# Joint block transposes, GpSimd reciprocals and a head-by-head latent layer in a four-layer transformer kernel

## The chip, the cores and the metric

The kernel runs on one core of a Trainium2 chip. The metric is the device time of one execution in microseconds (us); the time of a kernel is the median of its runs. The engines are named as the profile names them: PE (TensorE, matmuls), PEld (its weight loads), DVE (VectorE), ACT (ScalarE), POOL (GpSimd) and SP (SyncE, which here only issues DMAs).

## The reference, cut to what matters

Two sequences of 1024 tokens with 128 features pass through four layers, each an attention and a feed-forward part with residuals, all in float32:

```python
x = x + attn_a(layernorm(x));  x = x + mx_ffn(layernorm(x))     # one shared key/value head, no mask
x = x + attn_b(layernorm(x));  x = x + mx_ffn(layernorm(x))     # 16 heads, causal
x = x + attn_c(layernorm(x));  x = x + moe(layernorm(x))        # latent keys/values of 32, causal
x = x + attn_d(layernorm(x));  x = x + moe(layernorm(x))        # 16 heads with biases, causal
# every attention: 16 heads of 64
attn = softmax(q @ k.T / 8, axis=-1);  out = (attn @ v) @ w_o
```

The softmax over the keys of each query is where the change lies: maximum, exponential with its sum, reciprocal of the sum, product with it, transpose, product with the values.

## The kernel before

**Units and steps.** The four layers are called a, b, c and d. A unit is one pair of heads of one batch, so each layer has 16 units. A unit is worked through in steps. In layer a a step is one tile of 128 queries against all 1024 keys (8 steps a unit, 128 in all). In the causal layers a step holds one or two query tiles whose keys together fill 1024 columns or fewer, in the order `[7], [6, 0], [5, 1], [4, 2], [3]` (5 steps a unit, 80 a layer).

**One step.** `scores` (line 638) makes the scores of both heads in PSUM, with two buffers, one for each head; DVE reduces each to its negative maximum (`nmax`, L682); ACT takes the exponential with that bias into the tile `pr` and leaves the sums in `tot` (L693); DVE makes the reciprocals `rec` (L701); POOL multiplies the probabilities by them (L705); DVE transposes them in blocks of 32x32 into `slots` (L775); 16 DMAs (13 in layer a, where ACT and POOL copy three quarters) move the blocks between quarters of the partitions into `prT` (L750); PE multiplies with the values into `av` (L849, in layer c L844). Key tiles that are not block-transposed go through PE (`pp`, L792) and a copy on ACT (L793).

**Order.** Every engine's order is written by hand: the program is recorded in the order of a loop over steps, and each engine runs its instructions in that order. In the iteration of step j the loop does, in this order: the transposes of step j-2, with the normalisation (reciprocal and POOL products) of step j-1 put in after the first transpose; additions of finished outputs to x; scores, maxima and exponentials of step j; some of the next unit's projections; some of the "side" work (norms, feed-forward groups, the next layer's start); and four key tiles of the product with the values. On DVE this makes, for each step: transpose of head 0, reciprocals, transpose of head 1, two or four maxima. A query block's (256 queries) product with the values is released two iterations after its second transpose.

**PE's rows.** In layers a, b and d a product over 64 rows takes half of PE's rows, and each head's scores run as two streams side by side, head 0 first, then head 1. The latent layer's products are over 32 rows. There, four streams run side by side, two for each head, taken in turn, and the masks of both heads follow them:

```python
if latent:
    in_turn([half(h) for h in range(2) for half in (lower, upper)])
    for h in range(2):
        mask(h)
```

Of the kernel before, what the change touches and what calls it, by code (L numbers as in the profile page):

```python
# [9 lines left out]
F32 = mybir.dt.float32  # L10
# [26 lines left out]
def kernel(ctx: ExitStack, tc: tile.TileContext, a: dict, out: bass.AP):  # L37
# [68 lines left out]
    prT_four = probTp.tile([P, 2 * 4 * AB], F32, tag="prT_four", name="prT_four")  # L106
    latT_first = probTp.tile([P, S], F32, tag="latT", name="latT")


    stats = {}  # L110

# [149 lines left out]
    def moe_group(nm, b, g, last, xT, eng=nc.gpsimd, other=None):  # L261
# [3 lines left out]
        if other:  # L265
            xn = qkp.tile([P, TPB, D], F32, tag="qx", name=f"xn_{k}")
            hids = [
                probp.tile([P, 2, S], F32, tag="pr", name=f"hid_{k}_{n}").rearrange(
                    "p h (c q) -> p (h c) q", q=QB
                ) for n in range(2)  # L270
            ]
        else:
            xn = None
# [335 lines left out]
    def keys(u, qt):  # L609
        return qt + 1 if layers[u[0]]["causal"] else NT  # L610

    def step_of(u, qts):
        k = f"{tag_of(u)}_{qts[0]}"
        at = {}
        if len(qts) == 2:
            at = {qts[1]: 0, qts[0]: keys(u, qts[1]) * P}
        else:
            at = {qts[0]: QB - min(QB, keys(u, qts[0]) * P // 2)}
        pr = probp.tile([P, 2, S], F32, tag="pr", name=f"pr_{k}")
        tot = small.tile([P, 2, len(qts)], F32, tag="tot", name=f"tot_{k}")  # L620
        return dict(u=u, qts=qts, at=at, k=k, pr=pr, tot=tot)

    def scores(st):


        u, qts, at, k = st["u"], st["qts"], st["at"], st["k"]
        causal, latent = layers[u[0]]["causal"], layers[u[0]]["kind"] == "latent"
        sc = [ps_s.tile([P, 2 * QB], F32, tag="sc", name=f"sc_{k}_{h}") for h in range(2)]

        def operands(h, half):  # L630
            if latent:
                return QUARTERS[2 * h + half], qT[u][0], kT[u]
            x = 1 if h != half else 0
            return ROWS[half], qT[u][x], kT[u][x]

        def product(h, half, qt, k0, k1, diagonal):
            r, q, kk = operands(h, half)
            yield nc.tensor.matmul(  # L638
                sc[h][:, at[qt] + k0 : at[qt] + k1], lhsT=q[r, qt * P : (qt + 1) * P],
                rhs=kk[r, k0:k1], start=True, stop=not diagonal,  # L640
            )
            d = at[qt] + qt * P
            for f in range(P // DH if diagonal and not latent else 0):
                yield nc.tensor.matmul(  # L644
                    sc[h][:, d + f * DH : d + P], lhsT=unit[r, f, :], rhs=over[r, f, f * DH :],
                    start=False, stop=(f == P // DH - 1),
                )

        def mask(h):

            for qt in reversed(qts):
                d = at[qt] + qt * P
                nc.tensor.matmul(  # L653
                    sc[h][:, d : d + P], lhsT=ident_b, rhs=over_all, start=False, stop=True
                )

        def lower(h):

            yield from product(h, 0, qts[0], 0, QB - at[qts[0]], False)
            if len(qts) == 2:  # L660
                yield from product(h, 0, qts[1], 0, keys(u, qts[1]) * P, True)

        def upper(h):
            mid = QB - at[qts[0]]
            yield from product(h, 1, qts[0], mid, keys(u, qts[0]) * P, causal)

        def in_turn(gens):
            while gens:
                gens = [g for g in gens if next(g, None) is not None]

        if latent:
            in_turn([half(h) for h in range(2) for half in (lower, upper)])
            for h in range(2):
                mask(h)
        nmaxs = []
        for h in range(2):
            if not latent:
                in_turn([lower(h), upper(h)])
            nmax = small.tile([P, len(qts)], F32, tag="nmax", name=f"nmax_{k}_{h}")
            for n, qt in enumerate(qts):  # L680
                c = slice(at[qt], at[qt] + keys(u, qt) * P)
                nc.vector.tensor_reduce(  # L682
                    out=nmax[:, n : n + 1], in_=sc[h][:, c], axis=AX.X, op=ALU.max, negate=True
                )
            nmaxs.append(nmax)
        return sc, nmaxs

    def exponentials(st, h, sc, nmax):

        u, tot = st["u"], st["tot"]  # L690
        for n, qt in enumerate(st["qts"]):
            c = slice(st["at"][qt], st["at"][qt] + keys(u, qt) * P)
            nc.scalar.activation(  # L693
                st["pr"][:, h, c], sc[:, c], AF.Exp, bias=nmax[:, n : n + 1],
                accum_out=tot[:, h, n : n + 1],
            )

    def normalize(st):
        u, pr = st["u"], st["pr"]
        rec = small.tile([P, 2, len(st["qts"])], F32, tag="rec", name=f"rec_{st['k']}")  # L700
        nc.vector.reciprocal(out=rec, in_=st["tot"])  # L701
        for h in range(2):
            for n, qt in enumerate(st["qts"]):
                c = slice(st["at"][qt], st["at"][qt] + keys(u, qt) * P)
                nc.gpsimd.tensor_scalar(  # L705
                    out=pr[:, h, c], in0=pr[:, h, c], scalar1=rec[:, h, n : n + 1], scalar2=1.0,
                    op0=ALU.mult, op1=ALU.mult,
                )

# [26 lines left out]
    def blocks_moved(u, qb):  # L736


        t, src = prT_of(u, qb)[:, : 2 * blocked(u, qb) * AB], blocks_of(u, qb)
        n = src.shape[1] // 4  # L740
        def ends(i, r):
            return t[QUARTERS[r], i * n : (i + 1) * n], src[QUARTERS[i], r * n : (r + 1) * n]

        copied = (1, 2, 3) if layers[u[0]]["kind"] == "shared" else ()
        for i, r in MOVES:
            if i != r or i not in copied:
                o, x = ends(i, r)
                nc.sync.dma_start(out=o, in_=x)  # L750
        for i in copied:
            o, x = ends(i, i)
            if i < 3:
                nc.gpsimd.tensor_scalar(
                    out=o, in0=x, scalar1=1.0, scalar2=1.0, op0=ALU.mult, op1=ALU.mult
                )
            else:
                copies.append((o, x))
        probT[u, qb] = t.rearrange("p (i t h c) -> p t h i c", t=TPA, h=2, i=4)

    def transposes(st):

        u, pr = st["u"], st["pr"]
        for qt in st["qts"]:
            qb, cols = qt // TPA, slice(qt % TPA * P, (qt % TPA + 1) * P)
            nk, nb = keys(u, qt), blocked(u, qb)
            for h in range(2 if nb else 0):
                n = min(nk, nb)  # L770
                dst = blocks_of(u, qb).rearrange(
                    "p (r t h k q) -> p t h k r q", r=4, t=TPA, h=2, q=32
                )[:, qt % TPA, h, :n]
                src = pr[:, h, st["at"][qt] : st["at"][qt] + n * P]
                nc.vector.transpose(  # L775
                    dst,
                    src.rearrange("p (k r q) -> p k r q", r=4, q=32),
                )
                yield
            if nb < nk and nb:  # L780
                o = rest_of(u, qb)[:, qt % TPA].unsqueeze(2)
            elif nb < nk:
                if (u, qb) not in probT:
                    probT[u, qb] = prT_of(u, qb).rearrange("p (h k q) -> p h k q", h=2, q=AB)
                o = probT[u, qb][:, :, :, cols]
            for k0 in range(nb, nk, 2):
                k1 = min(k0 + 2, nk)
                pt = ps_m.tile([P, 2, 2, P], F32, tag="pm", name=f"pp_{tag_of(u)}_{qt}_{k0}")
                for h in range(2):
                    for kt in range(k0, k1):  # L790
                        c0 = st["at"][qt] + kt * P
                        nc.tensor.transpose(pt[:, h, kt - k0, :], pr[:, h, c0 : c0 + P], ident)  # L792
# [11 lines left out]
    def weigh(u, qb, bank, kt, ends):  # L804
# [12 lines left out]
        def moving(h, kt, t0, t1=TPA):  # L817
# [5 lines left out]
            cols = slice(kt * 32, (kt + 1) * 32)  # L823
            return x[:, :, cols] if t1 - t0 == 1 else x[:, :, :, cols]

        def shaped(o, t0, t1=TPA):
            if not blocked(u, qb):
# [405 lines left out]
```

## Time and profile before

| | |
|---|---|
| median of 3 runs | 2314.12 us (2311.34 to 2315.66) |
| span of the profiled execution, first to last instruction | 2309.5 us; its own total is not given apart, the runs stand 1.8 to 6.2 us above it |
| PE busy | 2112.7 us (91%) |
| DVE busy | 1716.0 us (74%) |
| ACT busy | 1491.3 us (65%) |
| POOL busy | 1285.7 us (56%) |
| DMAs `prT<-slots` | 768 of 128 KB, 832 of 112 KB, 768 of 96 KB |

By the first and the last product of scores the layers lie at 20 to 681 us (a), 685 to 1181 us (b), 1183 to 1669 us (c) and 1673 to 2226 us (d). Busy time counts an instruction from its start to its end; matmuls are pipelined, so a busy PE need not be full. DMA issues on SP count as no busy time.

### The profile page before, as it was taken

What the parts mean: (1) busy time and instruction counts of PE and PEld (TensorE: products, weight loads), DVE (VectorE), ACT (ScalarE), POOL (GpSimd) and SP (SyncE); (2) the same over time, 40 slices, a digit from 0 to 9 for tenths busy, and PEclk for the clock granted to TensorE, in tenths of its full rate; (3) what the DMA queues carried; (4) which work ended last, traced back from release to release, by engine and by line L of the source; (5) the groups of instructions that cost most, each with busy time, mean ns of one, the idle gap of its engine ahead of it and who ended that gap; (6) DMA issues with size and microseconds to landing.
All of it is one profiled execution on the core that took longest, in us unless ns stands there. A gap on an engine that the chain in (4) does not pass through costs nothing.

```text
span 2309.5 us, 43436 instructions
## 1 busy us (share of the span) xinstructions
PE 2112.7 (91%) x14833; PEld 1232.0 (53%) x14833; DVE 1716.0 (74%) x2695; ACT 1491.3 (65%) x3340; POOL 1285.7 (56%) x1723
## 2 busy tenths in 40 slices
PE   6999999999998999999987897888889999999986
PEld 2454444444445666666654454444455666656653
DVE  7978999999986876678668877776666566766544
ACT  5777777767765666666665566656666557666552
POOL 4756767767765454455545645555644446544441
PEclk9999999999999999999998889899899999999997
DMA  5666666556676666666655556544665546646450
GB/s 139 145 150 151 154 150 149 135 131 153 149 189 153 151 154 161 164 153 156 150 130 121 121 128 146 130 104 111 162 156 131 125 114 156 162 118 145 110 135 10
DMA packets 144635, 320.45 MB, mean 139 GB/s; under 512 B 48288, under 2 KB 58784, under 8 KB 144416
## 3 DMA queue, kind: packets, MB, share of 16 engines
q1 hardware_dynamic: 144416, 317.67, 58.2%
q8 instruction: 120, 1.97, 0.4%
q14 instruction: 99, 0.81, 0.1%
HBM read 10.27 MB, written 2.10 MB: 5 GB/s over the span
## 4 chain that ended last, share of the span: by engine, by line
PE 49%; DVE 15%; SPq 12%; ACT 10%; DMA 5%; issue 5%; POOL 3%; DVEq 0%; ACTq 0%; POOLq 0%
SPq L750 12%; PE sc_a L638 5%; PE av_a L849 4%; PE av_d L849 4%; DVE slots L775 4%; DMA prT<-slots 4%; PE sc_b L638 4%; PE av_b L849 4%; PE sc_d L638 4%; DVE nmax_a L682 3%; ACT pr_a L693 3%; ACT pr_c L693 3%; PE sc_c L638 3%; DVE nmax_d L682 2%; DVE nmax_c L682 2%
## 5 line engine op out<-in xcount | busy, mean ns | idle before, releaser
L693 ACT ACTIVATE pr_a<-sc_a,nmax_a 128x1024 f32<-128x1024 f32 x256 | 283.2, 1111 | 169.9 <-DVE nmax_a L682 168.0
L705 POOL TENSOR_SCALAR pr_a<-pr_a,rec_a 128x1024 f32<-128x1024 f32 x256 | 284.1, 1123 | 192.9 <-DVE rec_a L701 192.6
L705 POOL TENSOR_SCALAR pr_d<-pr_d,rec_d 128x1024 f32<-128x1024 f32 (+7 forms) x256 | 186.9, 750 | 269.0 <-DVE rec_d L701 268.8
L682 DVE TENSOR_REDUCE nmax_a<-sc_a 128x1 f32<-128x1024 f32 x256 | 298.3, 1204 | 28.0 <-PE sc_a L638 27.6
L705 POOL TENSOR_SCALAR pr_b<-pr_b,rec_b 128x1024 f32<-128x1024 f32 (+7 forms) x256 | 187.3, 752 | 219.9 <-DVE rec_b L701 219.5
L705 POOL TENSOR_SCALAR pr_c<-pr_c,rec_c 128x1024 f32<-128x1024 f32 (+7 forms) x256 | 187.5, 753 | 206.4 <-DVE rec_c L701 206.4
L682 DVE TENSOR_REDUCE nmax_d<-sc_d 128x1 f32<-128x1024 f32 (+7 forms) x256 | 177.1, 747 | 150.2 <-PE sc_d L644 150.2
L693 ACT ACTIVATE pr_c<-sc_c,nmax_c 128x1024 f32<-128x1024 f32 (+7 forms) x256 | 186.5, 739 | 153.5 <-DVE nmax_c L682 123.9
L693 ACT ACTIVATE pr_b<-sc_b,nmax_b 128x1024 f32<-128x1024 f32 (+7 forms) x256 | 186.5, 739 | 146.8 <-DVE nmax_b L682 130.3
L638 PE MATMUL sc_a<-k_a,q_a 64*128 64x512 f32 x512 | 266.8, 631 | 15.0 <-ACT pr_a L693 14.2
L775 DVE STREAM_TRANSPOSE slots<-pr_a 128x896 f32<-128x896 f32 x256 | 278.8, 1093 | 1.7 <-DMA prT<-slots 1.3
L693 ACT ACTIVATE pr_d<-sc_d,nmax_d 128x1024 f32<-128x1024 f32 (+7 forms) x256 | 186.6, 739 | 135.0 <-DVE nmax_d L682 129.5
L638 PE MATMUL sc_a<-k_a,qx_a 64*128 64x512 f32 x512 | 264.1, 631 | 0.0
L682 DVE TENSOR_REDUCE nmax_b<-sc_b 128x1 f32<-128x1024 f32 (+7 forms) x256 | 176.6, 745 | 89.0 <-PE sc_b L644 88.9
L682 DVE TENSOR_REDUCE nmax_c<-sc_c 128x1 f32<-128x1024 f32 (+7 forms) x256 | 176.8, 747 | 84.8 <-PE sc_c L653 84.0
L849 PE MATMUL av_a<-prT,v_a 128*64 128x256 f32 x1792 | 221.4, 386 | 7.5 <-DMA prT<-slots 5.2
L849 PEld LDWEIGHTS av_a<-prT,v_a 128*64 128x64 f32 x1792 | 121.1, 136 | 122.3 <-issue 69.0
L638 PE MATMUL sc_d<-k_d,q_d 64*128 64x512 f32 (+3 forms) x416 | 159.9, 497 | 0.3 <-ACT pr_d L693 0.3
L638 PE MATMUL sc_b<-k_b,q_b 64*128 64x512 f32 (+3 forms) x416 | 159.1, 495 | 1.1 <-ACT pr_b L693 1.1
L638 PE MATMUL sc_d<-kx_d,qx_d 64*128 64x512 f32 (+3 forms) x416 | 154.3, 490 | 0.2
L638 PE MATMUL sc_b<-kx_b,qx_b 64*128 64x512 f32 (+3 forms) x416 | 153.5, 488 | 0.7 <-ACT pr_b L693 0.6
L775 DVE STREAM_TRANSPOSE slots<-pr_b 128x1024 f32<-128x1024 f32 (+3 forms) x128 | 130.5, 1024 | 9.6 <-DMA prT<-slots 9.0
(408 smaller groups left out, 4782.3 us busy)
## 6 DMA issues: line engine op xcount, KB each, us to landing
prT<-slots SPq DMA_DIRECT2D x768, 128.0 KB, 2.3
prT<-slots SPq DMA_DIRECT2D x832, 112.0 KB, 2.2
prT<-slots SPq DMA_DIRECT2D x768, 96.0 KB, 2.1
qx_b<-q_b SPq DMA_DIRECT2D x32, 256.0 KB, 3.5
kx_b<-k_b SPq DMA_DIRECT2D x32, 256.0 KB, 3.4
qx_d<-q_d SPq DMA_DIRECT2D x32, 256.0 KB, 3.6
kx_d<-k_d SPq DMA_DIRECT2D x32, 256.0 KB, 3.5
x<-in_x SPq DMA_DIRECT2D x4, 256.0 KB, 3.7
```

What stands on the lines that cost most here:

```text
L638: yield nc.tensor.matmul(sc[h][:, at[qt] + k0 : at[qt] + k1], lhsT=q[r, qt * P : (qt + 1) * P], rhs=kk[r, k0:k1], start=True, stop=not dia ...
L682: nc.vector.tensor_reduce(out=nmax[:, n : n + 1], in_=sc[h][:, c], axis=AX.X, op=ALU.max, negate=True)
L693: nc.scalar.activation(st["pr"][:, h, c], sc[:, c], AF.Exp, bias=nmax[:, n : n + 1], accum_out=tot[:, h, n : n + 1],)
L705: nc.gpsimd.tensor_scalar(out=pr[:, h, c], in0=pr[:, h, c], scalar1=rec[:, h, n : n + 1], scalar2=1.0, op0=ALU.mult, op1=ALU.mult,)
L750: nc.sync.dma_start(out=o, in_=x)
L775: nc.vector.transpose(dst, src.rearrange("p (k r q) -> p k r q", r=4, q=32),)
L849: nc.tensor.matmul(shaped(av[ROWS[h], n], t0), lhsT=vs[u][:, kt, h, :], rhs=moving(h, kt, t0), start=(kt == 0), stop=(kt == nkt - 1),)
```

## The change

The probabilities of both heads lie interleaved by key tile in `pr` (`[P, key tile, head, 128]` in place of `[P, head, 1024]`). One DVE instruction transposes both heads of a query tile; it replaces two. The reciprocals are made on POOL, as the sums to the power of -1, against a constant tile of -1; the DVE instruction goes away. In the latent layer each head's scores run as two streams on two quarters of PE's rows, followed by that head's mask, and then the other head. The values' product reads its blocks at other strides. The numbers of DMAs, matmuls and exponentials are the same.

```diff
+    minus = const.tile([P, 4], F32, tag="minus", name="minus")
+    nc.gpsimd.memset(minus, -1.0)
...
-        pr = probp.tile([P, 2, S], F32, tag="pr", name=f"pr_{k}")
+        pr = probp.tile([P, NT, 2, P], F32, tag="pr", name=f"pr_{k}")
...
-        if latent:
-            in_turn([half(h) for h in range(2) for half in (lower, upper)])
-            for h in range(2):
-                mask(h)
         nmaxs = []
         for h in range(2):
-            if not latent:
-                in_turn([lower(h), upper(h)])
+            in_turn([lower(h), upper(h)])
+            if latent:
+                mask(h)
...
+    def tiles_of(st, qt):
+        t0 = st["at"][qt] // P
+        return st["pr"][:, t0 : t0 + keys(st["u"], qt)]
...
             nc.scalar.activation(
-                st["pr"][:, h, c], sc[:, c], AF.Exp, bias=nmax[:, n : n + 1],
-                accum_out=tot[:, h, n : n + 1],
+                tiles_of(st, qt)[:, :, h, :], sc[:, c].rearrange("p (k q) -> p k q", q=P),
+                AF.Exp, bias=nmax[:, n : n + 1], accum_out=tot[:, h, n : n + 1],
             )
...
-        nc.vector.reciprocal(out=rec, in_=st["tot"])
+        nc.gpsimd.tensor_tensor(
+            out=rec, in0=st["tot"],
+            in1=minus[:, : 2 * len(st["qts"])].rearrange("p (h n) -> p h n", h=2), op=ALU.pow,
+        )
         for h in range(2):
             for n, qt in enumerate(st["qts"]):
-                c = slice(st["at"][qt], st["at"][qt] + keys(u, qt) * P)
+                pt = tiles_of(st, qt)[:, :, h, :]
                 nc.gpsimd.tensor_scalar(
-                    out=pr[:, h, c], in0=pr[:, h, c], scalar1=rec[:, h, n : n + 1], scalar2=1.0,
+                    out=pt, in0=pt, scalar1=rec[:, h, n : n + 1], scalar2=1.0,
                     op0=ALU.mult, op1=ALU.mult,
                 )
...
-            for h in range(2 if nb else 0):
+            tiles = tiles_of(st, qt)
+            if nb:
                 n = min(nk, nb)
                 dst = blocks_of(u, qb).rearrange(
-                    "p (r t h k q) -> p t h k r q", r=4, t=TPA, h=2, q=32
-                )[:, qt % TPA, h, :n]
-                src = pr[:, h, st["at"][qt] : st["at"][qt] + n * P]
+                    "p (r t c q) -> p t c r q", r=4, t=TPA, q=32
+                )[:, qt % TPA, : 2 * n]
                 nc.vector.transpose(
                     dst,
-                    src.rearrange("p (k r q) -> p k r q", r=4, q=32),
+                    tiles[:, :n].rearrange("p k h (r q) -> p (k h) r q", q=32),
                 )
                 yield
```

More of the change, by code (lines that the diff above doesn't have):

```diff
@@ L267, in moe_group @@
             hids = [
-                probp.tile([P, 2, S], F32, tag="pr", name=f"hid_{k}_{n}").rearrange(
-                    "p h (c q) -> p (h c) q", q=QB
+                probp.tile([P, NT, 2, P], F32, tag="pr", name=f"hid_{k}_{n}").rearrange(
+                    "p (c n) h q -> p c (n h q)", c=2 * NQB
                 ) for n in range(2)
@@ L693, in exponentials @@
             nc.scalar.activation(
-                st["pr"][:, h, c], sc[:, c], AF.Exp, bias=nmax[:, n : n + 1],
-                accum_out=tot[:, h, n : n + 1],
+                tiles_of(st, qt)[:, :, h, :], sc[:, c].rearrange("p (k q) -> p k q", q=P),
+                AF.Exp, bias=nmax[:, n : n + 1], accum_out=tot[:, h, n : n + 1],
             )
     def normalize(st):
-        u, pr = st["u"], st["pr"]
         rec = small.tile([P, 2, len(st["qts"])], F32, tag="rec", name=f"rec_{st['k']}")
-        nc.vector.reciprocal(out=rec, in_=st["tot"])
+        nc.gpsimd.tensor_tensor(
+            out=rec, in0=st["tot"],
+            in1=minus[:, : 2 * len(st["qts"])].rearrange("p (h n) -> p h n", h=2), op=ALU.pow,
+        )
         for h in range(2):
             for n, qt in enumerate(st["qts"]):
-                c = slice(st["at"][qt], st["at"][qt] + keys(u, qt) * P)
+                pt = tiles_of(st, qt)[:, :, h, :]
                 nc.gpsimd.tensor_scalar(
-                    out=pr[:, h, c], in0=pr[:, h, c], scalar1=rec[:, h, n : n + 1], scalar2=1.0,
+                    out=pt, in0=pt, scalar1=rec[:, h, n : n + 1], scalar2=1.0,
                     op0=ALU.mult, op1=ALU.mult,
@@ L758, in blocks_moved @@
                 copies.append((o, x))
-        probT[u, qb] = t.rearrange("p (i t h c) -> p t h i c", t=TPA, h=2, i=4)
+        probT[u, qb] = t.rearrange("p (i t k h q) -> p t h i k q", t=TPA, h=2, i=4, q=32)
     def transposes(st):
-        u, pr = st["u"], st["pr"]
+        u = st["u"]
         for qt in st["qts"]:
@@ L790, in transposes @@
                     for kt in range(k0, k1):
-                        c0 = st["at"][qt] + kt * P
-                        nc.tensor.transpose(pt[:, h, kt - k0, :], pr[:, h, c0 : c0 + P], ident)
+                        nc.tensor.transpose(pt[:, h, kt - k0, :], tiles[:, kt, h, :], ident)
                 nc.scalar.copy(o[:, :, k0 - nb : k1 - nb], pt[:, :, : k1 - k0, :])
@@ L822, in moving @@
             x = probT[u, qb][:, t0, h] if t1 - t0 == 1 else probT[u, qb][:, :, h]
-            cols = slice(kt * 32, (kt + 1) * 32)
-            return x[:, :, cols] if t1 - t0 == 1 else x[:, :, :, cols]
+            return x[:, :, kt] if t1 - t0 == 1 else x[:, :, :, kt]
         def shaped(o, t0, t1=TPA):
```

## The prediction

> **What bounds the kernel now.** I read the page first, then windows of single units, the list of waits, and last the timelines of one step in layers a and c.
>
> ```profile
> span 2309.5 us, 43436 instructions
> PE 2112.7 (91%) x14833; PEld 1232.0 (53%) x14833; DVE 1716.0 (74%) x2695; ACT 1491.3 (65%) x3340; POOL 1285.7 (56%) x1723
> ```
>
> PE is busy for 91%, so at most some 197 us are to be had from the whole program unless PE's own work changes. Where the gap lies is told by windows, each about one unit of layers a (plain), a (with norms and feed-forward rounding on DVE beside it), b and c:
>
> ```profile
> core 0: us, PE busy (x) PEld busy (x) DVE busy (x) ACT busy (x) POOL busy (x), PEclk, DMA share, GB/s
> 274.30:313.70 39.40, 37.72 (x230) 18.42 (x228) 35.86 (x40) 30.15 (x55) 27.67 (x26) 1.00 0.66 152
> 395.20:440.50 45.30, 41.60 (x244) 19.43 (x245) 43.79 (x55) 30.76 (x56) 32.69 (x40) 1.00 0.57 132
> 911.40:940.70 29.30, 28.64 (x222) 19.17 (x220) 19.38 (x29) 19.91 (x52) 14.29 (x19) 1.00 0.69 162
> 1395.70:1422.50 26.80, 21.66 (x201) 11.48 (x194) 19.38 (x29) 17.81 (x47) 14.29 (x19) 1.00 0.61 141
> ```
>
> A plain unit of a leaves PE 1.7 us idle, one with side work 3.7 us with DVE 97% busy, b 0.7 us, c 5.1 us. Layer b is bound by PE, and d like it (484 of 500 us in its window 1720:2220); a is bound by DVE with PE close behind; c by neither. The timeline of a plain step of a, DVE alone:
>
> ```profile
> 309.00 0.17 DVE L701 RECIPROCAL rec_a<-tot_a 128x2 f32<-128x2 f32 x1 [0.28 <-ACT pr_a L693]
> 309.08 1.09 DVE L775 STREAM_TRANSPOSE slots<-pr_a 128x896 f32<-128x896 f32 x1
> 310.09 2.32 DVE L682 TENSOR_REDUCE nmax_a<-sc_a 128x1 f32<-128x1024 f32 x2
> 312.33 1.09 DVE L775 STREAM_TRANSPOSE slots<-pr_a 128x896 f32<-128x896 f32 x1
> 313.71 0.17 DVE L701 RECIPROCAL rec_a<-tot_a 128x2 f32<-128x2 f32 x1 [0.28 <-ACT pr_a L693]
> ```
>
> From reciprocal to reciprocal 4.71 us: the reciprocal waits for ACT's last sum, and the second transpose and the maxima wait behind it in DVE's order. So maximum, two exponentials, reciprocal, transpose, maximum are one loop. In c the timeline of PE and DVE shows another:
>
> ```profile
> 1406.97 1.13 PE L638 MATMUL sc_c<-latT,q_c 32*128 32x128 f32 x4 [0.54 <-ACT pr_c L693]
> 1408.31 1.13 PE L638 MATMUL sc_c<-latT,q_c 32*128 32x128 f32 x8 [0.21 <-ACT pr_c L693]
> 1409.37 0.40 PE L653 MATMUL sc_c<-over_all,ident_b 128*128 128x128 bf16 x4
> 1409.70 2.48 DVE L682 TENSOR_REDUCE nmax_c<-sc_c 128x1 f32<-128x640 f32 x4 [0.23 <-PE sc_c L653]
> ```
>
> Head 0's first products start once its PSUM buffer is free, but the next ones in the turn are head 1's, whose buffer is read by ACT until 1408.25. All the rest, both masks too, stands behind that, so DVE gets head 0's scores at 1409.70 although its buffer was free at 1406.92. Products, masks, maxima and exponentials run one after the other: 5.6 us a step.
>
> **The change part by part.** All sums are made against this execution: span 2309.5, to which the median run adds 4.6 us lying around it.
>
> *Joint transposes and no reciprocal on DVE.* L775 takes 1.09 us for 896 columns and 1.225 for 1024, so 1.05 ns a column and 0.15 us fixed, 0.08 of it not hidden by the next instruction. One of 1792 takes 2.02 us; a merged pair saves 0.08. In a step of a the reciprocal's 0.08, its 0.28 wait and the 0.08 after the first transpose's end go too: DVE's step falls from 4.71 to 2.24 (maxima) + 1.95 = 4.2 us. What is late next is PE: 37.7 us a unit, and the DMAs. From the end of a block's second transpose there are 13 issues, whose records start 0.635 us apart, 2.2 us to the landing of the last and 0.3 to PE's first matmul: 10.15 us. Now that transpose ends on average 1.6 us after PE starts the step's scores; joint, it starts right after the maxima and ends 0.9 us earlier. Two steps later PE has done 1.9 us of scores first, so two steps cannot take less than 0.7 + 10.15 - 1.9 = 8.95 us, against 8.3 of PE's own work where no projection lies between. I add 0.5 a unit for this: 38.2. Eleven plain units gain 1.2 each (13 us); four with side work gain 8 x 0.44 = 3.5 on DVE, of which PE leaves 2.5 (10 us); the first two 2. Layer a: **25 us**. In b and d DVE idles for PE anyway; PE's idle 16 + 16 us lie in DMA waits and side work: **5 us**. Waiting for both heads costs nothing while POOL has ended: in a POOL's products end 0.86 us before the first transpose starts.
>
> *Reciprocals on POOL.* 368 instructions on 128x2 or 128x4 (128 in a, 240 in b to d). No row shows a power. From below, the same kind of instruction with a multiply, from the list of the line that norms use on both engines:
>
> ```profile
> L142 DVE TENSOR_TENSOR lnt_a<-lny_a x3: 166/166/170, 8.3 to 9.9; 128x8 f32<-128x8 f32 x3
> L142 POOL TENSOR_TENSOR lnt_a<-lny_a x3: 200/203/206, 81.9 to 91.9; 128x8 f32<-128x8 f32 x3
> ```
>
> so 0.2 us; no row of POOL is shorter, which excludes a gain. From above, the norms' inverse root, which POOL makes of 12 such instructions: 2.4 us. I take 0.35: it is one instruction of the lower row's kind on fewer columns with more arithmetic in each, and nearer to that row. It costs nothing then: now POOL starts 0.29 us after ACT's last sum (313.68 to 313.97), with the power 0.5, and POOL's busy time in a plain unit of a rises from 27.7 to 30.5 of 38. Queued behind it are the products, POOL's copies of blocks and additions to x; the joint transpose waits for the products. It is free as long as 27.7 + 8X stays under 38.2, X under 1.3 us. The Trainium skill ("GPSIMD Engine Reference", section Engine selection) speaks against it: it calls POOL about twice as slow as DVE in two-input work. The rows say 203 against 166 ns; by the page's factor the power would take an estimated 0.33 us and the sum would be the same.
>
> *Interleaved tile.* Exponentials and products write 8 runs of 128 in place of 1024 in a row. No row shows it for these; v's copy on ACT, into a tile of two heads, takes 0.61 us for 512 columns against 0.59 for a plain one. Below, 0; above, 3% of 470 us of exponentials in a and 3% of POOL's; both lie beside PE and DVE. I take 0.
>
> *Layer c, head by head.* Head 0's scores and mask no longer wait for head 1's buffer: in the step shown they could end at 1408.1 and DVE start, after its joint transpose, at 1408.5 in place of 1409.7. The 5.6 us loop opens, and PE is next. Two streams a head, masks included, take b 2.17 us for both heads (912.98 to 915.15 in PE's timeline); c's now fill 0.5 + 1.3. So PE gets 0.4 more a step, 2 a unit: 21.7 becomes 23.7 in the unit shown. The DMAs bind first: 16 issues are 15 x 0.635 + 2.5 = 12.0 us, and from their end to the next transpose of tile 6 lie products with values 1.1, PE transposes 1.1, scores 2.2, projection and values 2.2, scores of one head 1.1, maxima 2.5, transpose 2.0: 24.2 a unit. Plain units, 26.7 on average, come to 25.0: ten times 1.7 are 17 us; the six with side work (29 to 38 us) gain 1 each, 6. PE's granted clock is 0.92 in the window 1200:1640, so some 35 us pass for lack of it; a PE that idles less may win back between 0 and 10, I take 5. Layer c: **28 us**. A rule that speaks against it is in the Trainium skill, "TensorEngine Tiling (Array Packing)", section When to Use Tiling: with 32 rows to contract, pack four. By it nothing should be gained, and doubled streaming is an estimated 0.85 us a step lost; the trace agrees on the streams (1.06 us for four against 2.17), but shows four of them waiting 1.34 us for one buffer.
>
> **Sum.** 25 + 5 + 28 = 58 us, were each layer to reach its next bound. Layer b, which is bound by PE, still loses 1 us a unit against it (16 us in 460). I take as much off c's 16 units; a's new bound already holds 0.5 a unit. 42 us remain: span 2267.5, time 2272.
>
> **The rivals.** *The power is dear (slower).* No row shows what a power costs. At 2.4 us POOL needs 46.9 us in a plain unit of a against 39.4: +7.5 x 16 = 120. In b and d a step's loop over two steps (transpose 2.2, maxima 2.5, exponentials 1.7, power, products 2.7, 0.2 of waits) grows to 11.7, 5.85 a step against 5.4: some 20 more; c keeps 10 of its gain. About 2444. It decides from 1.5 us on, where POOL's 27.7 + 8X passes the unit of now; the whole turns slower at 1.7. For it: only the far row bounds it. Against: 2 or 4 columns. *PE and the DMAs hold a as it is.* PE is 96% busy there; if its fill can't rise, a gives a few us and c 15: 2294. Against: b runs at 98%. *Two streams eat c's gain.* If the six side-work units are bound by PE, each pays 2 to 4 us, and the plain ones gain nothing: c +20, a and b to d -20: 2314. Against: those units leave PE 4 to 6 us idle. *The change does not do what it says* can be excluded for the order: DVE has 320 transposes in place of 640, and no reciprocals in the steps.
>
> **How the numbers follow.** The forecast (2240 to 2288) has 0.56, a held as it is 0.14, c's streams 0.10 (0.06 no change, 0.04 slower), the dear power 0.20. A measurement of this kernel tells 0.2% from no change, 2309.5 to 2318.7. Faster 0.70, same 0.06, slower 0.24. The range reaches from 2240, where nearly the whole 58 us and a free power come true, to 2335, over the second and third rival and a power of some 1.8 us; what lies past it is the dearer powers, 0.16, and 0.04 below.
>
> **What would show it.** Right: L775's successor with a mean near 2.0 us for 1792 columns; the power under 0.5 us on POOL; DVE in a waiting for PE scores in place of ACT; a plain unit of a near 38.2 us with PE over 97%; in c the first maximum right after its transpose, units near 25 us. Wrong: POOL's power over 1 us and DVE's transposes waiting for POOL products; more waits of PE for `prT` in a; PE busy in c over 27 us a unit.

## The result and the profile after

| | before | changed |
|---|---|---|
| median | 2312.73 us (4 runs) | 2335.91 us (4 runs, 2329.32 to 2341.57) |
| ratio, 95% interval | | 1.0092, 1.0066 to 1.0119 |
| span of the profiled execution | 2309.5 us | 2335.0 us |

The change makes the kernel slower by 0.9%; 2272 us were forecast. The page of the changed kernel:

```profile
span 2335.0 us, 43762 instructions
PE 2180.8 (93%) x14833; PEld 1260.5 (54%) x14833; DVE 1671.7 (72%) x2007; ACT 1496.3 (64%) x3340; POOL 1597.0 (68%) x2092
```

DVE lost 44 us of work, as meant. But PE is 68 us busier with the same 14833 matmuls, and POOL 311 us busier. From the first reciprocal (or power) of each layer to the next layer's, layer a takes 665.3 us (663.7 before), b 497.9 (498.3), c 509.4 (489.6), d with the tail 636.3 (632.0). So a's and d's forecast gains did not come, and c lost 20 us in place of gaining 28 (12 after the 16 us that the prediction's sum takes off again). Windows of the changed kernel, a plain unit each of a, b and c, the same units as before, with the busy time of each engine:

```profile
core 0: us, PE busy (x) PEld busy (x) DVE busy (x) ACT busy (x) POOL busy (x), PEclk, DMA share, GB/s
273.90:312.70 38.80, 37.98 (x230) 18.41 (x232) 34.40 (x25) 30.23 (x55) 33.35 (x34) 1.00 0.69 155
912.40:941.60 29.20, 29.11 (x228) 19.53 (x224) 18.56 (x20) 19.98 (x51) 18.76 (x25) 1.00 0.71 164
1402.60:1432.30 29.70, 27.88 (x198) 14.20 (x194) 18.81 (x20) 18.07 (x47) 18.74 (x24) 0.84 0.55 124
```

The plain unit of a did get shorter (39.4 to 38.8), b's stayed, c's went from 26.8 to 29.7: PE 6 us busier in it, and its granted clock at 0.84. The groups of the power on POOL (busy us, mean ns) show the first reason:

```profile
L704 POOL TENSOR_TENSOR rec_a<-tot_a,minus 128x2 f32<-128x2 f32 x128 | 91.6, 716 | 89.5 <-ACT pr_a L697 55.9 <-PE av_a L853 19.4 <-PE pp_a L797 2.8
L704 POOL TENSOR_TENSOR rec_c<-tot_c,minus 128x4 f32<-128x4 f32 x48 | 49.3, 1028 | 89.6 <-ACT pr_c L697 76.8 <-DVE slots L781 12.1 <-DVE bst_c L126 0.8
```

0.72 us for two columns and 1.03 for four, against the 0.35 that was taken. And it is waited for. DVE's timeline in a:

```profile
312.23 2.05 DVE L781 STREAM_TRANSPOSE slots<-pr_a 128x1792 f32<-128x1792 f32 x1 [0.85 <-POOL pr_a L711]
314.20 2.31 DVE L682 TENSOR_REDUCE nmax_a<-sc_a 128x1 f32<-128x1024 f32 x2
316.44 2.03 DVE L781 STREAM_TRANSPOSE slots<-pr_a 128x1792 f32<-128x1792 f32 x1
319.00 2.36 DVE L682 TENSOR_REDUCE nmax_a<-sc_a 128x1 f32<-128x1024 f32 x2 [0.54 <-PE sc_a L641]
```

The loop of the step is what was forecast (2.0 and 2.24 us, and PE is waited for). New is the 0.85 us in which the joint transpose waits for POOL's products. The sums, from the list of DVE's waits (us in total, times, longest):

```profile
DVE slots L781 <- POOL pr_a L711: 24.1, 35, 2.7
DVE slots L781 <- POOL pr_c L711: 22.2, 18, 4.2
...
DVE slots L781 <- POOL pr_d L711: 14.2, 17, 4.3
```

Before, the only such line is 2.1 us in c. The second reason is in PE's timeline in c, in the unit of the window above:

```profile
1407.77 1.08 PE L536 MATMUL pq_c<-xT,wq_c 128*128 128x512 f32 x2
...
1422.17 0.66 PE L874 MATMUL po_c<-wo_c,attnT_c 128*128 128x128 f32 x4
1423.41 0.44 PE L797 MATMUL pp_c<-ident,pr_c 128*128 128x128 f32 x2 [0.58 <-POOL pr_c L711]
1424.75 0.65 PE L797 MATMUL pp_c<-ident,pr_c 128*128 128x128 f32 x4 [0.90 <-POOL pr_c L711]
1425.33 1.91 PE L641 MATMUL sc_c<-latT_c,q_c 32*128 32x512 f32 x4
...
1427.39 2.08 PE L641 MATMUL sc_c<-latT_c,q_c 32*128 32x512 f32 x4
...
1429.48 2.02 PE L536 MATMUL pq_c<-xT,wq_c 128*128 128x512 f32 x2
```

PE waits twice for POOL's products in query tile 2, and from 1425.5 us on everything takes about twice as long for 6.8 us: the projection `pq` 2.02 us against 1.08 in the view's first line. The granted clock is at one half in that stretch. Over all of layer c it was at one half for 109.2 us, before for 88.7.

### The profile page after: what moved, and what is told of

It reads as the page before. It is cut to its first block, busy times and chain, and to the rows that moved or that the text cites. A ratio compares the mean times of both kernels' runs of the same rounds, so it can differ in the third digit from the quotient of the medians.

```text
span 2335.0 us, 43762 instructions
## 1 busy us (share of the span) xinstructions
PE 2180.8 (93%) x14833; PEld 1260.5 (54%) x14833; DVE 1671.7 (72%) x2007; ACT 1496.3 (64%) x3340; POOL 1597.0 (68%) x2092
## 4 chain that ended last, share of the span: by engine, by line
PE 53%; POOL 17%; DVE 10%; issue 8%; SPq 6%; ACT 4%; DMA 3%; POOLq 0%; DVEq 0%; ACTq 0%
PE sc_a L641 6%; SPq L756 6%; PE av_d L853 5%; PE av_a L853 5%; PE sc_d L641 4%; PE av_b L853 4%; PE sc_b L641 4%; POOL pr_c L711 4%; POOL pr_a L711 4%; PE sc_c L641 3%; DVE nmax_d L682 2%; DMA prT<-slots 2%; DVE slots L781 2%; PE pp_d L797 2%; DVE nmax_c L682 1%
## 5 line engine op out<-in xcount | busy, mean ns | idle before, releaser
L697 ACT ACTIVATE pr_a<-sc_a,nmax_a 128x1024 f32<-128x1024 f32 x256 | 283.1, 1111 | 169.5 <-DVE nmax_a L682 165.8
L682 DVE TENSOR_REDUCE nmax_a<-sc_a 128x1 f32<-128x1024 f32 x256 | 298.9, 1206 | 52.1 <-PE sc_a L641 46.5
L711 POOL TENSOR_SCALAR pr_a<-pr_a,rec_a 128x1024 f32<-128x1024 f32 x256 | 284.6, 1124 | 13.0
L697 ACT ACTIVATE pr_c<-sc_c,nmax_c 128x1024 f32<-128x1024 f32 (+7 forms) x256 | 187.1, 740 | 157.3 <-DVE nmax_c L682 136.5
L781 DVE STREAM_TRANSPOSE slots<-pr_a 128x1792 f32<-128x1792 f32 x128 | 260.8, 2037 | 26.1 <-POOL pr_a L711 24.1
L682 DVE TENSOR_REDUCE nmax_c<-sc_c 128x1 f32<-128x1024 f32 (+7 forms) x256 | 182.3, 750 | 123.0 <-PE sc_c L656 112.0
L704 POOL TENSOR_TENSOR rec_d<-tot_d,minus 128x4 f32<-128x4 f32 (+1 forms) x80 | 71.6, 896 | 193.4 <-ACT pr_d L697 183.3
L704 POOL TENSOR_TENSOR rec_b<-tot_b,minus 128x4 f32<-128x4 f32 (+1 forms) x80 | 73.2, 916 | 142.5 <-ACT pr_b L697 140.8
L704 POOL TENSOR_TENSOR rec_c<-tot_c,minus 128x4 f32<-128x4 f32 (+1 forms) x80 | 72.7, 909 | 141.6 <-ACT pr_c L697 119.8
```

Of the source, the lines that this page charges most:

```text
L682: nc.vector.tensor_reduce(out=nmax[:, n : n + 1], in_=sc[h][:, c], axis=AX.X, op=ALU.max, negate=True)
L697: nc.scalar.activation(tiles_of(st, qt)[:, :, h, :], sc[:, c].rearrange("p (k q) -> p k q", q=P), AF.Exp, bias=nmax[:, n : n + 1], accum_o ...
L704: nc.gpsimd.tensor_tensor(out=rec, in0=st["tot"], in1=minus[:, : 2 * len(st["qts"])].rearrange("p (h n) -> p h n", h=2), op=ALU.pow,)
L711: nc.gpsimd.tensor_scalar(out=pt, in0=pt, scalar1=rec[:, h, n : n + 1], scalar2=1.0, op0=ALU.mult, op1=ALU.mult,)
L781: nc.vector.transpose(dst, tiles[:, :n].rearrange("p k h (r q) -> p (k h) r q", q=32),)
```

## The experiments

The expectations of the first four runs call them by these names. **Theory 1:** the two streams a head are the loss: they cost PE work that layer c has no room for, and PE's clock falls behind them. **Theory 2:** the power is the loss: its duration lies between the last exponential and the products, and both the joint transposes and PE's transposes wait for the products. The third part, the joint transposes, was expected to gain under both; only **Theory 3** makes it the loss, as a joint transpose waits for the products of both heads.

All the runs in one table: ratio to the kernel before, run on the same chip, with its interval; then, of the profiled execution, the span, the layers as cut above, and the half-clock time in c.

| kernel | median | ratio (95%) | span | a | b | c | d | half clock in c |
|---|---|---|---|---|---|---|---|---|
| before | 2312.7 to 2317.1 | 1 | 2309.5 | 663.7 | 498.3 | 489.6 | 632.0 | 88.7 |
| changed (all three parts) | 2335.9 | 1.0092 (1.0066 to 1.0119) | 2335.0 | 665.3 | 497.9 | 509.4 | 636.3 | 109.2 |
| joint transposes alone | 2294.4 | 0.9908 (0.9890 to 0.9925) | 2294.1 | 658.0 | 497.9 | 485.8 | 625.6 | 85.3 |
| power alone | 2324.0 | 1.0042 (1.0027 to 1.0057) | 2319.4 | 664.7 | 495.3 | 498.0 | 634.5 | 102.4 |
| streams alone | 2328.6 | 1.0063 (1.0042 to 1.0084) | 2324.6 | 663.9 | 495.6 | 503.2 | 635.2 | 92.2 |
| joint + power | 2328.9 | 1.0058 (1.0042 to 1.0075) | 2324.5 | 665.2 | 499.0 | 498.0 | 634.6 | 92.2 |
| joint + streams | 2296.7 | 0.9936 (0.9916 to 0.9955) | 2295.2 | 660.1 | 495.7 | 486.2 | 626.5 | 68.3 |
| joint + a multiply for the power | 2297.0 | 0.9926 (0.9911 to 0.9940) | 2297.1 | 653.8 | 494.4 | 487.0 | 634.0 | 95.6 |
| joint + power twice | 2411.3 | 1.0421 (1.0408 to 1.0435) | 2411.9 | 701.3 | 511.0 | 529.5 | 642.6 | 136.5 |
| joint, reciprocals first | 2454.8 | 1.0604 (1.0588 to 1.0620) | 2446.9 | 749.3 | 516.7 | 505.6 | 647.8 | 93.6 |
| joint + power head by head in b to d | 2328.5 | 1.0058 (1.0044 to 1.0072) | 2322.1 | 656.4 | 505.8 | 496.9 | 636.7 | 105.8 |
| changed + 160 matmuls in c | 2325.2 | 1.0041 (1.0028 to 1.0055) | 2324.2 | 668.5 | 497.2 | 501.0 | 630.1 | 30.7 |
| joint + streams in 8 units | 2290.6 | 0.9899 (0.9883 to 0.9915) | 2285.7 | 657.6 | 496.5 | 478.3 | 626.3 | 58.0 |
| the same + 160 matmuls in c | 2296.9 | 0.9913 (0.9899 to 0.9926) | 2295.2 | 659.4 | 493.8 | 489.2 | 626.0 | 44.4 |

### The parts, one by one

*Joint transposes alone* is the changed kernel with

```diff
-        nc.gpsimd.tensor_tensor(out=rec, in0=st["tot"], in1=minus[...], op=ALU.pow)
+        nc.vector.reciprocal(out=rec, in_=st["tot"])
```

and with layer c's four streams and their order taken from the kernel before:

```diff
+        if latent:
+            in_turn([half(h) for h in range(2) for half in (lower, upper)])
+            for h in range(2):
+                mask(h)
         nmaxs = []
         for h in range(2):
-            in_turn([lower(h), upper(h)])
-            if latent:
-                mask(h)
+            if not latent:
+                in_turn([lower(h), upper(h)])
```

> Joint transposes on the interleaved tile alone; reciprocals stay on DVE, behind the joint transpose, and layer c keeps four streams. Of the 23 us that the whole change cost, layer c holds 20 (489.6 to 509.4 us). Theory 1, two streams and the slower clock behind them: this part is free of both, and gives what layer a gave in plain units (39.4 to 38.9 us) or more, since the reciprocal no longer waits: 8 to 20 us under the kernel before. Theory 2, the power on GpSimd: the same sign and size, so this run alone does not tell them apart; it tells what the joint transpose is worth. Theory 3, that DVE's wait for both heads' products costs: 5 to 15 us over the kernel before, with transposes in c waiting for POOL.

Measured 2294.4 us, 0.92% faster than before: by themselves the joint transposes gain about 21 us, just over the 8 to 20 expected, and Theory 3 is out.

*Power alone* is the kernel before with the first diff turned round (and the constant tile); *streams alone* is the kernel before with the second turned round; *joint + power* is the changed kernel with the second diff.

> The kernel before with the reciprocals as powers on POOL, split transposes, four streams in c. Theory 1: within 5 us of the kernel before, since the power's 0.72 or 1.03 us lies beside other work. Theory 2: 10 to 25 us over it, PE's transposes of c waiting for POOL products over 60 us in place of 43 (both rows of the list of waits).

> The kernel before with layer c head by head on two quarters, nothing else. Theory 1 (two streams cost PE more than the opened loop gives, and PE's clock falls more often): 12 to 25 us over the kernel before, PE busy in plain units of c at 26 to 28 us in place of 22 to 24, half-clock time in c over the 89 us of before. Theory 2 (the power's late products make PE wait, and the wait halves the clock): 0 to 20 us under the kernel before, units of c near 25 to 26 us.

> The changed kernel with four streams put back in layer c. Theory 1: c returns to 485 to 492 us and the whole to 2305 to 2316. Theory 2: c stays over 500 us and the whole within 8 us of the changed kernel (2336).

Measured: the power by itself costs 0.42% (9 to 10 us: over Theory 1's 5, just under Theory 2's 10 to 25), the streams by themselves 0.63% (Theory 1's 12 to 25 us). On top of the joint transposes the power costs 34.5 us (2294.4 to 2328.9). The two profiled executions lie 30.4 us apart: 7 in a, 1 in b, 12 in c, 9 in d. The whole gain of the joint transposes goes, and more. Read the other way round, beside the power the joint transposes gain nothing (2324.0 and 2328.9 us; layer a 664.7 and 665.2). On top of these two, the streams cost 7 us more by the medians and 10.5 by the spans, but the two ratios' intervals overlap. Layer c with joint transposes and the power, 498.0 us, lies between what the two theories expected for it. The power has the larger share of the loss; of the streams it is shown only that they cost something by themselves.

*Joint + streams* is the changed kernel with the first diff.

> The changed kernel with the reciprocals left on DVE: joint transposes and two streams a head in layer c. Theory A (the two streams cost PE work of their own, whatever else is changed): layer c alone gets longer than with joint transposes and four streams, by 10 to 18 us, and PE's busy time in c rises from 411 to some 465 us; 2305 to 2312 us, a ratio near 0.997. Rival B (the streams hurt only beside the power, or are hidden beside the joint transposes): within 4 us of the joint transposes alone, 2292 to 2298 us.

Measured 2296.7 us, and layer c 486.2 against 485.8 us without the streams: with DVE's reciprocals the two ratios lie 0.28% apart, their intervals overlap, and c itself stays as it was. Theory A's 10 to 18 us in c did not come, although PE's busy time there did rise, from 411 to 447 us. What this hides is shown by single units (windows below). So the power is needed for the changed kernel to be slower: without it, it is faster than before by 0.4 to 0.8%.

### Is it the power's arithmetic or its place?

*A multiply for the power:* the changed kernel with four streams and a multiply in the power's place. It leaves out the reciprocals, so its results are not the softmax; only its time is of use.

```diff
-    nc.gpsimd.memset(minus, -1.0)
+    nc.gpsimd.memset(minus, 0.001)
...
-            in1=minus[...], op=ALU.pow,
+            in1=minus[...], op=ALU.mult,
```

> Joint transposes, four streams, and on POOL in the power's place a multiply of the same operands (the constant is 0.001), so the reciprocals are left out. Theory A (the power's arithmetic is the cost: 0.72 and 1.03 us where a multiply should take some 0.2): of the 34.5 us that the power adds to the joint transposes no more than 0.2/0.9 remains, so 2292 to 2303 us, and layer c is back at 486 to 490. Rival B (the cost is the place, an instruction more in POOL's queue ahead of the products): 2318 us or more, as with the power (2329).

*Power twice:* the changed kernel with four streams, and the instruction of the power written a second time behind the first.

> Joint transposes, four streams, and the power issued twice on POOL, one after the other, each writing the same reciprocals. Theory A (each microsecond of the power stands in the chain from the exponentials to the transposes): once more the 34.5 us, and more in layer a, where POOL with 33.4 + 5.8 = 39.2 us a unit passes the unit's 38.8: 2360 to 2390 us. Rival B (the first power already pushed the products behind a point, and more of it is covered): 2328 to 2345 us.

Measured 2297.0 and 2411.3 us, with 2328.9 for one power between them. The second is 21 us more than Theory A expected. The multiply's groups on POOL:

```profile
L707 POOL TENSOR_TENSOR rec_a<-tot_a,minus 128x2 f32<-128x2 f32 x128 | 25.7, 200 | 143.1 <-ACT pr_a L700 87.8 <-PE av_a L856 32.6 <-PE sc_a L641 7.3
L707 POOL TENSOR_TENSOR rec_c<-tot_c,minus 128x4 f32<-128x4 f32 x48 | 9.7, 202 | 122.7 <-ACT pr_c L700 122.7
```

At 0.20 us the same instruction in the same place costs nothing that can be told from DVE's reciprocals (0.9926 against 0.9908, intervals overlapping); layer a is even 4 us shorter, and d 8 longer. For the whole kernel the duration is what counts, not the place. Layer d is the exception: of the 9 us that the power adds there, 8.4 come with the multiply already, and why stays open. The price is not in proportion: from the multiply to the power 32 us, from one power to two 82. DVE's waits for POOL's products show why. In a, with joint transposes, by the list of DVE's waits of each kernel, first DVE's reciprocals, then the multiply, one power and two:

```profile
DVE slots L778 <- POOL pr_a L708: 8.3, 23, 1.9
```

```profile
DVE slots L784 <- POOL pr_a L714: 4.3, 5, 2.0
```

```profile
DVE slots L784 <- POOL pr_a L714: 22.3, 28, 2.7
```

```profile
DVE slots L788 <- POOL pr_a L718: 76.7, 70, 3.3
```

In c it goes 6.4 (multiply), 16.8 and 45.6 us. The first power still fits into the time that many steps have to spare ahead of the transpose; the second finds little left: in layer a the joint transpose starts within 0.1 us of the end of the products that it needs in 16 of 128 steps with the multiply, in 44 with one power and in 80 with two.

The power alone, in the kernel before, cost only 10 us. Two things differ there. A transpose of head 0 needs only head 0's products, and DVE's transposes wait for POOL for 4.2 us in a and 7.2 us in c. And the power takes the reciprocal and its wait off DVE, which the joint transposes had done without it: seven plain units of a (the 4th to 8th, 14th and 15th) average 39.4 us before, 38.8 with the power alone, 38.5 with joint transposes alone and 38.9 with both. No run tells how much of the larger price beside joint transposes is owed to each.

### Where the reciprocals stand

In the four units of layer a with side work, joint transposes alone gained nothing (176.6 us together, 174.9 before), and PE waits 21.2 us in a for POOL's products, before 5.8. *Reciprocals first* tried to start the products sooner; it is the kernel of joint transposes alone with

```diff
-            for _ in transposes(st):
-                if last_step:
-                    normalize(last_step.pop())
+            if last_step:
+                normalize(last_step.pop())
+            for _ in transposes(st):
+                pass
```

> Joint transposes, four streams, DVE reciprocals, but the reciprocals of step j-1 are made ahead of the joint transpose of step j-2 and not behind it. Theory A (in the units of layer a with side work, where PE waits 16 us more for POOL's products than before, it is the reciprocal behind a 2 us transpose that starts the products late): PE's waits for POOL in a fall from 21 to under 10 us, a from 658 to 645 to 652, in all 2278 to 2288 us. Rival B (the reciprocal waits for ACT's last sum and holds the transpose and the maxima behind it): plain units of a get 0.3 us a step longer, 38.4 to 40 us or more, 2296 to 2315 us.

Measured 2454.8 us. Rival B had the direction and not the size: plain units of a take 46.5 us in place of 38.4. DVE's timeline in one:

```profile
330.93 0.17 DVE L704 RECIPROCAL rec_a<-tot_a 128x2 f32<-128x2 f32 x1 [1.30 <-ACT pr_a L697]
331.01 2.02 DVE L778 STREAM_TRANSPOSE slots<-pr_a 128x1792 f32<-128x1792 f32 x1
332.96 2.31 DVE L682 TENSOR_REDUCE nmax_a<-sc_a 128x1 f32<-128x1024 f32 x2
336.57 0.17 DVE L704 RECIPROCAL rec_a<-tot_a 128x2 f32<-128x2 f32 x1 [1.30 <-ACT pr_a L697]
```

With no transpose between the maxima and the reciprocal, DVE stands still through head 1's exponential: 5.64 us a step. PE's waits for POOL in a all but vanish (1.5 us), as they would if the late reciprocal was their cause, but a loop that is slower altogether hides such waits too, and PE's waits for ACT ahead of the scores grow to 77.3 us (1.7 before the move). The multiply above speaks for that cause more plainly: with the instruction on POOL, behind no transpose, PE waits 4.0 us in a for POOL's products, and the four units take 172.9 us. The timeline shows what the joint transpose gains in a plain unit: it covers that whole exponential (4.2 us of DVE a step), where one head's transpose covered all but 0.28 us of it (4.71).

*Power head by head:* if the power's place in the chain is the cost, head 0's can be made beside head 1's exponential.

```diff
+        if u[0] == 0:
+            nc.vector.reciprocal(out=rec, in_=st["tot"])
         for h in range(2):
+            if u[0]:
+                nc.gpsimd.tensor_tensor(
+                    out=rec[:, h], in0=st["tot"][:, h], in1=minus[:, :nq], op=ALU.pow
+                )
```

> Joint transposes, four streams; in layer a the reciprocals stay on DVE, in b to d the power on POOL is made head by head: head 0's in front of head 0's products, head 1's in front of head 1's. That is 160 powers a layer more or less halved in width in place of 80, by the durations of 128x2 and 128x4 (0.72 and 1.03 us) some 105 us of POOL a layer where the undivided ones took 72. Theory A (what costs is the power's place in the chain from the last exponential to the transposes, and head 0's now runs beside head 1's exponential): layer a as with joint transposes alone (658), b to d shorter than with the undivided power (b 499, c 498, d 635), c 486 to 494; in all 2295 to 2312 us. Rival B (what costs is POOL's busy time): b to d longer than with the undivided power, c 500 to 512; in all 2325 us or more.

Measured 2328.5 us; a 656.4 as expected, but b 505.8, c 496.9, d 636.7 against 499.0, 498.0 and 634.6 with the undivided power. Theory A's gain in b to d did not come; c is shorter by 1 us and b longer by 7, as POOL's busy time (366 us in b, 333 undivided) would have it. So splitting it did not hide the power: two of 0.71 us on 128x2 take more than one of 1.03 on 128x4. What the earlier start gave and what the 33 us more took can't be told apart by this run.

### The streams and PE's clock

Scores of layer c alone (PE busy, PEld, DVE, ACT): a unit with side work and the clock at 1.00, first of the kernel before, then of streams alone:

```profile
1511.60:1546.60 35.00, 7.39 (x68) 2.86 (x52) 11.06 (x16) 12.11 (x32) 1.00 0.43 101
```

```profile
1523.10:1558.30 35.20, 12.04 (x68) 4.90 (x52) 11.46 (x16) 12.17 (x32) 1.00 0.44 101
```

The same 68 matmuls take 4.65 us more. The unit itself is only 0.2 us longer, as PE's idle time in it falls from 4.5 to 1.2 us. In a plain unit at full clock (1395.7 to 1422.5 us of the kernel before, 1367.0 to 1391.7 of joint + streams) it is 9.62 against 12.04:

```profile
1395.70:1422.50 26.80, 9.62 (x68) 3.41 (x52) 11.05 (x16) 12.11 (x32) 1.00 0.61 141
```

```profile
1367.00:1391.70 24.70, 12.04 (x68) 4.91 (x52) 11.40 (x16) 12.22 (x32) 1.00 0.63 144
```

Four streams take about 2 us more there than in the unit with side work, with their waits inside the turn. So the two streams cost 2.4 us of PE's time where PE had idle time between, and 4.65 where it had other work. The whole plain unit of joint + streams:

```profile
1367.00:1391.70 24.70, 22.40 (x184) 12.59 (x184) 19.23 (x26) 17.96 (x47) 14.29 (x19) 1.00 0.63 144
```

24.7 us: the forecast's 25.0, and 5 us shorter than the changed kernel's unit. By units, cut at the reciprocals, the eight of c with little side work (the 1st, 6th to 11th and 16th) take 214 us together with joint + streams, 225 with joint transposes alone and 230 before; the other eight 272, 260 and 260. So the forecast gain is there, and side work takes it back. With streams alone both groups are longer than before, 235 and 269 us: the gain comes only together with the joint transposes. The plain unit of the changed kernel holds the same instructions, but for the reciprocals. What differs is the waits for POOL (0.76 us in one place against 0.58 + 0.90) and the clock, which falls behind the longer ones.

To see how the two hang together, I cut layer c of fourteen profiled executions (all of the table) into the stretches of 3.41 us in which the clock is granted (in layer c of each it keeps a value for a multiple of this time), and asked of each full-clock stretch how long PE ran no matmul in it and what clock came next:

| PE idle in 3.41 us | next at full clock | next at half |
|---|---|---|
| under 0.3 | 960 | 0 |
| 0.3 to 0.9 | 315 | 23 |
| 0.9 to 1.5 | 171 | 85 |
| 1.5 to 2.1 | 21 | 52 |
| over 2.1 | 0 | 44 |

*Changed + 160 matmuls* tests whether the idle time is the cause:

```diff
                 for h in range(2):
+                    for _ in range((4, 6)[h] if layers[u[0]]["kind"] == "latent" and (qt, k0) == (2, 0) else 0):
+                        nc.tensor.matmul(pt[:, h, 0, :], lhsT=ident, rhs=ident, start=True, stop=True)
                     for kt in range(k0, k1):
                         nc.tensor.transpose(pt[:, h, kt - k0, :], tiles[:, kt, h, :], ident)
```

> The changed kernel with ten matmuls of 128x128 more in each unit of layer c (160 in all, results overwritten): four ahead of the transposes of head 0 of query tile 2 and six ahead of those of head 1, the two places where PE waits 0.6 and 0.9 us for POOL's products and after which its granted clock is halved for 6.8 or 10.2 us. Theory A (a stretch of 3.4 us in which PE idles for about a microsecond or more brings the halved clock in the next one): PE's half-clock time in c falls from 109 us to 60 to 85, the plain units from 29.7 to 25.5 to 27, and the time by 8 to 25 us to 2311 to 2328, though PE has some 22 us more to do. Rival B (the halved clock has nothing to do with these waits): half-clock time in c stays at 100 or more, and the time stays or grows, 2334 to 2360 us.

Measured 2325.2 us, 11 less than without: more work, less time. Half-clock time in c falls from 109.2 to 30.7 us, more than the 60 to 85 of Theory A, and in the 6th to 9th unit from 36 us to none. A plain unit's window, and PE's timeline at the place shown above:

```profile
1402.40:1428.70 26.30, 25.26 (x212) 15.03 (x211) 18.81 (x20) 17.91 (x47) 18.68 (x24) 1.00 0.62 140
```

```profile
1420.61 1.06 PE L797 MATMUL pp_c<-ident 128*128 128x128 f32 x8
1421.50 0.38 PE L799 MATMUL pp_c<-ident,pr_c 128*128 128x128 f32 x2
1421.72 1.50 PE L797 MATMUL pp_c<-ident 128*128 128x128 f32 x12
1423.06 0.60 PE L799 MATMUL pp_c<-ident,pr_c 128*128 128x128 f32 x4
1423.59 0.70 PE L641 MATMUL sc_c<-latT_c,q_c 32*128 32x512 f32 x2
```

The added matmuls fill the two waits, the clock stays at 1.00, and the unit takes 26.3 us in place of 29.7. Here the idle time is shown to be the cause of the halved clock, not only to go with it. The Trainium skill ("TensorE: Matmul & The Clock Gate", Part 1) describes such a gate, with free-running windows of 3413 ns and the slow state after an idle window. The runs agree on the window's length; on the condition they differ: 1.5 to 2.1 us of idle time in 3.41 brought the half clock 52 times in 73.

### A version that is faster than both

*Joint + streams in 8 units* is joint + streams, with four streams kept where side work fills PE:

```diff
+    PLAIN = {(0, 0), (0, 5), (0, 6), (0, 7), (1, 0), (1, 1), (1, 2), (1, 7)}
...
+        split = latent and u[1:] in PLAIN
+        if latent and not split:
+            in_turn([half(h) for h in range(2) for half in (lower, upper)])
+            for h in range(2):
+                mask(h)
         nmaxs = []
         for h in range(2):
-            in_turn([lower(h), upper(h)])
-            if latent:
+            if not latent or split:
+                in_turn([lower(h), upper(h)])
+            if split:
                 mask(h)
```

> Joint transposes, DVE reciprocals; two streams a head only in the eight units of layer c (the 1st, 6th to 11th and 16th) that carry little side work, four streams in the other eight. Theory A (the two streams pay where PE would idle and cost where side work already fills PE): c takes the shorter of the two units each time, by the units of the two runs before some 11 us less than with four streams everywhere: c 474, in all 2280 to 2288 us. Rival B (the units run into one another and the clock moves with them, so that the units cannot be picked one by one): within 4 us of the joint transposes alone, 2291 to 2298 us.

Measured 2290.6 us, between the two expectations. In the profiled executions c is 478.3 us, 7.5 less than with four streams everywhere (11 expected): the eight units with two streams take 217 us (225 with four), the other eight 261 (260), as Theory A has it. The kernel is 1.0% faster than before, but by the medians only 3.8 us ahead of joint transposes alone, and the two intervals overlap, so a gain over those is not shown. The last run adds the 160 matmuls to it:

> The kernel with joint transposes, DVE reciprocals and two streams in eight of c's units, and besides the ten overwritten matmuls a unit of layer c. Theory A (they keep PE from idling and so the clock up in the units where it still falls): half-clock time in c from 58 to under 40 us and c from 478 to 468 to 476; 2278 to 2288 us. Rival B (its plain units are at full clock already and its other units wait for POOL for 3 to 5 us, too long for 1.5 us of matmuls to bridge): the half-clock time stays within 10 us of 58, and the 160 matmuls cost 0 to 10 us: 2288 to 2300 us.

Measured 2296.9 us, c 489.2: the time is Rival B's. The half-clock time fell from 58.0 to 44.4 us, more than Rival B's 10 and less than Theory A's 18, and PE's busy time in c rose by 30. Here the fill did not pay.

## Why the prediction was wrong

The forecast was faster (2272 us, with a chance of 0.70 for faster); it came out slower, at 2335.9 us, just past the upper end of the range.

- **The step that failed first is "Reciprocals on POOL": 0.35 us, "It costs nothing then".** Measured 0.72 us on 128x2 and 1.03 on 128x4: inside the bounds of 0.2 and 2.4, but twice and three times the value taken, which leaned on the multiply's row because the instruction was of the same kind. The width matters as well, which no bound allowed for.
- **The second half of that step is the worse one: "free as long as 27.7 + 8X stays under 38.2, X under 1.3 us".** It asks whether POOL has room in a unit. At 0.72 us POOL is busy for 33.35 of 38.8 us, by that rule free; beside the joint transposes the power cost 7.2 us in a all the same, and 34.5 in the whole, over half of the 64 us between forecast and result. What counted was the chain from the last exponential through the products to the transpose, and DVE's waits in it. The prediction had one number of it, the 0.86 us between POOL's last product and the transpose, and used it for "Waiting for both heads costs nothing". But that is one step of a plain unit: 0.72 us fits into it, and seven plain units of a lose only 0.3 us each. It did not ask how the steps stand in units with side work, where the price is paid: 6.1 us in the 2nd and 13th unit of a together, 4.9 in the 7th of d. The dear-power rival had the mechanism, "DVE's transposes waiting for POOL products" as its sign too, but put its threshold at 1.5 us. The runs put it above the multiply's 0.2 us and at or below the power's 0.72 to 1.03.
- **Joint transposes.** 2.04 us on average for 1792 columns (2.02 forecast) and 4.2 us of DVE a step: right. Plain units of a at 38.5 on average in place of 39.4 (38.2 forecast): right. The "four with side work" (10 us): wrong, they gained nothing, since with the reciprocal behind a transpose twice as long the products start a microsecond later (2.07 us after ACT's last sum on average in these units, before 1.07) and PE waits for them. The sum for a also counts 17 units (eleven, four and two) of 16. Layer a so gave 6 of 25 us, b and d 7 (5 forecast).
- **Interleaved tile.** Forecast 0: exponentials 1111 ns and products 1124 ns on 128x1024 in the changed kernel, as before. Right.
- **Layer c: "PE gets 0.4 more a step, 2 a unit", "the six with side work gain 1 each", "I take 5" for the clock.** In plain units the first is right, 2.4 us, and with DVE's reciprocals the 6th to 9th come to 24 to 26 us as forecast (25.0). In units with side work the price is 4.65 us of PE's time, 0.93 a step (near the 0.85 a step that the prediction estimated for doubled streaming and set aside; its 1.06 us for four streams has no masks in it, its 2.17 for two has), and by the units of joint + streams they lose 1.5 us each. The rival "two streams eat c's gain" named this, with a chance of 0.10. That its c (+20) came out is luck: with joint transposes, the two streams and no power c is 3.4 us shorter than before, and the 20 need both. The clock went the other way: 20 us more at half clock, where a gain was entered. Without the power the gain was there, 68.3 us in place of 88.7.
- **The terms were added as if apart.** They are not: the power takes the slack that the joint transposes need, and the waits that it makes bring the half clock back where the two streams had filled PE (in c 68.3 us with joint transposes and streams, 109.2 with the power as well). By itself each of the two slower parts costs 10 to 15 us; the joint transposes save 21; the three together cost 21.

## What to carry to other kernels

An instruction put between a producer and its waiting consumer is paid by the slack at that place, however idle its engine is over the stage; read the slack there step by step and subtract the new duration before anything else, in the tightest units as well as in the plain ones (here 0.86 us in the step that was read, and under 0.1 us in 16 of layer a's 128 steps with nothing but a multiply in the place). An operation with no row in the trace is not priced by its instruction's name: multiply and power were one kind of instruction here, 0.20 and 1.03 us on the same four columns. Where PE is the bound and its clock moves, a wait of a microsecond can cost more than its length (0.58 and 0.90 us here were followed by 6.8 us at half clock), so count half-clock time beside busy time.

## What the hardware showed that was not expected

- POOL's power: 0.72 us on 128x2 and 1.03 us on 128x4, while a multiply in its place takes 0.20 us on both.
- PE's clock: in layer c none of the 960 stretches of 3.41 us in which PE idled under 0.3 us was followed by half clock, and all 44 in which it idled over 2.1 us were. Ten added matmuls a unit (160 in all) took 78 us of half clock out of layer c and 11 us off the run.
- Four streams of 32 rows took 7.39 us for a unit's scores and masks, two streams a head 12.04 us, both at full clock: 1.6 times.
